# Delta times u in half units, read by groups of 32 rows

## The chip, the cores and the metric

The kernel runs on one core of one Trainium2 chip. The metric is the device time of one execution in microseconds; the time before is 8791.93 us, the median of three runs (8787.54 to 8800.51). A change of about 0.2% is what three such runs can tell from none.

## The reference

The input `x` is 4 images of 96 channels and 64 x 64 pixels, in float32. Four layers follow one another: a selective scan in four directions (layer 0), a deformable 3 x 3 convolution (layer 1), a Fourier mixing and a quantised feed-forward (layer 2), and linear attention with another feed-forward (layer 3). The change is in layer 0. Cut to what matters there:

```python
xs = stack(rows, columns, rows reversed, columns reversed)   # 4 directions k, 192 channels d, 4096 positions
delta = softplus(dts + delta_bias)                           # per k, d and position
def step(h, inp):                                            # h: 16 states n for each k, d
    d_t, u_t, b_t, c_t = inp
    dA = exp(d_t[..., None] * A)
    h = dA * h + (d_t * u_t)[..., None] * b_t[:, :, None, :]
    y = einsum('bkdn,bkn->bkd', h, c_t)
    return (h, y)
_, ys = lax.scan(step, h0, (dl, ul, bl, cl))
y = ys + D * u
```

So for each image, each of 4 directions and each of 192 channels, 16 linear recurrences run over 4096 positions. `delta * u` has one value per channel and position and has to reach all 16 states.

## The kernel before

Layer 0 first computes delta and delta times u for 512 positions at a time, 128 or 64 channels at a time (`steps`, L811 on), and stores them in DRAM (`de_d`, `du_d`). Delta times u is stored as three bfloat16 parts whose sum is the float32 value: L866, L871 and L876 make the parts with the help of two products with minus the identity, and L880 stores them as `[direction, part, channel, position]`.

The scan (`scan`, L884 on) reads them back. Its work is cut into 1536 units. A unit is one image, one direction, 1024 positions and 8 channels x 16 states on the 128 partitions. Eight units make a block of 64 channels (`i` from 0 to 3, `q` from 0 to 1: unit `s = i + 4q` has the 8 channels from `8s`), three blocks make a step, and four steps make an image's direction. For each unit:

- `fetch` (L948) loads delta, each of 8 rows of 4 KB read 16 times, into `da` (L979, from ScalarE's queue), five units ahead.
- `fetch_block` (L991) loads, once per block and some six units ahead, two tiles `du` of 96 partitions (3 parts x 32 channels) and 1024 positions from SyncE's queue (L994). `fetch_step` loads B and C as `bc` (L986).
- `decay` (L998): ScalarE makes exp(A delta) in place (L1000), with a column of `al` as scale.
- `inflow` (L1003): TensorE spreads delta times u over the states. The 96 rows of one `du` tile are multiplied with a matrix `rep` of zeros and ones, 96 x 128, which picks the unit's 8 of 32 channels and adds the 3 parts. Two products of 512 positions fill the two PSUM banks of `db` (L1006). There are two `db` tiles.
- `enter` (L1020): VectorE multiplies `db` by B; `recur` (L1028): VectorE scans; `weigh` (L1035, L1037): GpSimd keeps the last state and multiplies by C.
- `total` (L1056): for two units at a time, TensorE adds the 16 states of each channel with `fold` into `py`, 32 channels at a time; `settle` (L1067) copies `py` to `yb`, `store` (L1074) writes it to DRAM.

Each engine takes its instructions in program order. That order is made when the program is written out: `scan` lays down the units, and between two units a planner (`Clock`, `pipe`, `Stream`) puts in steps of side work: layer 0 of the next image, layers 1 to 3 of earlier ones. A step goes in when the planner's account of each engine says that there is room; the account uses planned costs, such as the 0.8 us of TensorE per unit in `inflow` (L1004). Image 0 is computed by rows first, and its scan starts as soon as the first 1024 positions are there.

DMAs of SyncE and of ScalarE use eight semaphores in turn, in program order; an issue waits until the DMA eight before it has landed.

Of the kernel before, what the change touches and what calls it, by code (L numbers as in the profile page):

```python
# [20 lines left out]
L = H * W  # L21
DI, NS, R, KG = 192, 16, 6, 4
D2 = DI - 128
T = 1024
# [20 lines left out]
def prepare(x, **w):  # L45
# [51 lines left out]
    dtp[64 : 64 + R + 1, 2:] = dtw[2:].transpose(2, 0, 1)  # L97
    a["dtw"] = dtp

    al = w["L0_conv_A_logs"].reshape(KG, DI // D8, D8, NS)  # L100
    a["al"] = c(al.transpose(3, 2, 0, 1).reshape(128, KG * DI // D8))

    ds = w["L0_conv_Ds"].reshape(KG, NG, 64).transpose(2, 1, 0)
    a["ds"] = c(np.concatenate([ds, ds]))
# [22 lines left out]
    for n in (2, 3):  # L127
# [14 lines left out]
    a["cen_c"] = wide(cen[128:], 256)  # L142

    p = np.arange(128)
    rep = (p[:, None, None] % 32 == 8 * np.arange(4)[None, :, None] + p[None, None] % 8).astype(f)
    a["rep"] = c(rep)
    a["fold"] = c(
        (p[:, None, None] % 8 + 8 * np.arange(4)[None, :, None] == np.arange(32)[None, None]).astype(f)
    )
    yy, xx = np.divmod(np.arange(L).reshape(32, 128).T, W)  # L150
    ki, kj = np.divmod(np.arange(9), 3)
# [372 lines left out]
class Unit:  # L524


    def __init__(self, b, k, step, g, i, q):
        self.b, self.k, self.step, self.g, self.i = b, k, step, g, i
        self.s = i + 4 * q
        self.back = k >= 2  # L530
        self.j = NT - 1 - step if self.back else step
        self.n = 8 * g + self.s
        self.key = f"{b}_{k}_{self.j}_{g}_{self.s}"
        self.first_of_block = i == 0 and q == 0
        self.first_of_step = self.first_of_block and g == 0
        self.ts = slice(self.j * T, (self.j + 1) * T)
        self.bc = self.du = None
# [5 lines left out]
class Layer0:  # L543
# [7 lines left out]
    def __init__(self, ctx, net, x1):  # L551
        self.net, self.x1 = net, x1
        tc, nc, ins = net.tc, net.nc, net.ins
        wp = ctx.enter_context(tc.tile_pool(name="l0w", bufs=1))
        for name in ("fold", "al", "ds"):
            setattr(self, name, net.load(name, wp))

        nc.scalar.activation(self.al, self.al, AF.Exp)
        nc.vector.tensor_scalar_mul(self.al, self.al, -1.0)

        dsum = wp.tile([128, NG], F32, name="dsum")
        nc.vector.reduce_sum(dsum, self.ds, axis=mybir.AxisListType.X)
        self.skip = wp.tile([128, NG, 128], F32, name="skip")
        for g in range(NG):
            nc.vector.tensor_scalar_mul(self.skip[:, g, :], net.ident, dsum[:, g : g + 1])

        self.wc_d = net.dram.tile([C, 9, 256], F32, name="wc_d")
        self.rep = wp.tile([128, 4, 128], BF16, name="rep16")
        self.minus = wp.tile([128, 128], BF16, name="minus")
        nc.vector.tensor_scalar_mul(self.minus, net.ident, -1.0)  # L570
        with tc.tile_pool(name="l0prep", bufs=1) as tp:
            nc.vector.tensor_copy(self.rep, net.load("rep", tp))
            w_in = net.load("w_in", tp)
            cw = tp.tile([C, 9, 256], F32, name="cwr")
            nc.sync.dma_start(cw, ins["cw"].partition_broadcast(C))
            nc.vector.tensor_mul(cw, cw, w_in[:, :256].unsqueeze(1).to_broadcast([C, 9, 256]))
            nc.sync.dma_start(self.wc_d, cw)
        dram = net.dram
        self.u_d = [dram.tile([DI, L], F32, name=f"u{b}") for b in range(B)]
        self.z_d = [dram.tile([DI, L], F32, name=f"z{b}") for b in range(B)]  # L580
        self.de_d = [dram.tile([KG, DI, L], F32, name=f"de{b}") for b in range(B)]
        self.du_d = [dram.tile([KG, 3, DI, L], BF16, name=f"du{b}") for b in range(B)]
        self.bc_d = [dram.tile([KG, 2 * NS, L], F32, name=f"bcd{b}") for b in range(B)]
        self.y_d = [dram.tile([KG, DI, L], F32, name=f"y{b}") for b in range(B)]
        self.sp = ctx.enter_context(tc.tile_pool(name="l0s", bufs=2))
        self.banks = ctx.enter_context(ExitStack())
        self.ps = self.banks.enter_context(tc.tile_pool(name="l0q", bufs=1, space=PSUM))


        self.ready, self.summed = set(), set()  # L590

        self.scanned = (0.0, 0.0)

        self.settled = 0.0
# [215 lines left out]
    def steps(self, b, ks, j, us, dtw, sm, xdbl):  # L810
# [65 lines left out]
        nc.scalar.copy(du[:, 2, :], pr)  # L876
        yield cost(pe=0.4, act=0.6)
        for p0, p1, k, c0 in parts:
            dst = self.du_d[b][k][:, c0 : c0 + p1 - p0, cs]
            nc.sync.dma_start(dst.rearrange("s c t -> c s t"), du[p0:p1])  # L880
        self.ready.update((b, k, both, j) for k in ks)
        yield wait(frees="du")

# [66 lines left out]
    def fetch(self, u, before):  # L950


        sp, nc = self.sp, self.net.nc
        b, k, j, g, ts = u.b, u.k, u.j, u.g, u.ts
        c0 = 64 * g
        halves = [slice(j * T + h * CH, j * T + (h + 1) * CH) for h in range(2)]
        if not u.first_of_step:
            u.bc = before.bc
        elif u.bc is None:
            self.fetch_step(u)  # L960
        if u.first_of_step and u.step == 0:
            u.state = sp.tile([128, DI // D8], F32, name=f"st{u.key}", tag="st")
        else:
            u.state = before.state
        if not u.first_of_block:
            u.du, u.sums = before.du, before.sums
        else:
            u.sums = {"add": None}
            if u.du is None:
                self.fetch_block(u)  # L970
        if u.i == 1 and u.s == 1 and (k == 0 or u.back):
            add = u.sums["add"] = sp.tile([128, CH], F32, name=f"ad{u.key}", tag="ad", bufs=1)
            src = self.y_d[b][k - 2] if u.back else self.u_d[b]
            for h in range(2):
                nc.scalar.dma_start(add[64 * h : 64 * h + 64], src[c0 : c0 + 64, halves[h]])
        self.net.clock.add(ACT, 0.6, self.scanned[1])
        u.da = sp.tile([128, T], F32, name=f"da{u.key}", tag="da", bufs=6)
        src = self.de_d[b][k][c0 + D8 * u.s : c0 + D8 * u.s + D8, ts]
        nc.scalar.dma_start(u.da, src.unsqueeze(0).to_broadcast([NS, D8, T]))  # L979

    def fetch_step(self, u):
# [5 lines left out]

    def fetch_block(self, u):

        u.du = []  # L990
        for q in range(2):  # L991
            t = self.sp.tile([96, T], BF16, name=f"du{u.key}_{q}", tag=f"du{q}")
            c0 = 64 * u.g + 32 * q
            self.net.nc.sync.dma_start(t, self.du_d[u.b][u.k][:, c0 : c0 + 32, u.ts])  # L994
            u.du.append(t)

    def decay(self, u):
        u.decayed = self.net.clock.add(ACT, 1.15, 0.0)  # L998
# [1 line left out]
        self.net.nc.scalar.activation(u.da, u.da, AF.Exp, scale=self.al[:, a : a + 1])  # L1000

    def inflow(self, u):
        u.spread = self.net.clock.add(PE, 0.8, self.scanned[1])  # L1003
        db = self.ps.tile([128, 2, CH], F32, name=f"db{u.key}", tag="db", bufs=2)  # L1004
        for h in range(2):
            self.net.nc.tensor.matmul(  # L1006
                db[:, h, :],
                lhsT=self.rep[:96, u.s % 4, :],
                rhs=u.du[u.s // 4][:, h * CH : (h + 1) * CH],
                start=True,  # L1010
                stop=True,
            )
        u.db = db.rearrange("p h t -> p (h t)")
# [848 lines left out]
```

## Time and profile before

| | us |
|---|---|
| median of the runs (lowest, highest) | 8791.93 (8787.54, 8800.51) |
| profiled execution, own time | 8796.72 |
| its span, first to last instruction | 8794.9 |
| VectorE busy | 6862.6 (78%) |
| TensorE busy | 6606.4 (75%) |
| GpSimd busy | 5603.0 (64%) |
| ScalarE busy | 4917.9 (56%) |
| mean granted TensorE clock | 0.813 |

The first unit's multiply starts at 198.3 us and the last scan ends near 7490 us; before it layer 0 of image 0 is prepared, after it the rest of layers 1 to 3 is left. The 1536 scans (L1028, forms with and without an initial state) take 2344 and 2285 ns each, the multiplies by B (L1020) 1213 ns, GpSimd's multiplies by C (L1037) 2386 ns, ScalarE's exponentials (L1000) 1146 ns. Idle time of an engine is put down to what ended it. The chain of work that ended last goes back from the last instruction, at each step to what released it.

### The profile page before, as it was taken

The numbers are of one execution on the slowest core, as the hardware profiler recorded it, in microseconds if no ns is written. First come the engines' busy times: TensorE is split into PE (matmuls) and PEld (weight loads), VectorE is DVE, ScalarE is ACT, GpSimd is POOL, SyncE is SP. The second block draws the span as 40 slices with busy tenths as digits, with TensorE's granted clock in tenths as the row PEclk, the third lists the DMA queues.
The fourth block names the chain that finished last, engine by engine and source line by source line (L and its number), as shares of the span: only waits on it lengthen the run. The fifth ranks groups of instructions, "written<-read, shape, count | busy, mean of one in ns | idle before, by whom it ended". The sixth has DMA issues, their size and how long they took to land.

```text
span 8794.9 us, 96335 instructions
## 1 busy us (share of the span) xinstructions
PE 6606.4 (75%) x31960; PEld 2922.3 (33%) x31960; DVE 6862.6 (78%) x5155; ACT 4917.9 (56%) x9030; POOL 5603.0 (64%) x4291
## 2 busy tenths in 40 slices
PE   6665877679677776877677687777768887779697
PEld 2211221123232322321222354322325552367283
DVE  2799989989798988778899887788887878367414
ACT  4554566546577776655666765345676665322323
POOL 0565666666588887656688886566888776167000
PEclk8876887779788777887778788877888887888887
DMA  3577677877788888777788888766888787255110
GB/s 87 165 199 191 180 194 216 213 185 196 197 234 238 234 225 211 188 186 190 213 237 223 233 221 195 184 167 181 217 209 224 210 219 165 62 164 174 28 52 11
DMA packets 775990, 1608.41 MB, mean 183 GB/s; under 512 B 247809, under 2 KB 339357, under 8 KB 773382
## 3 DMA queue, kind: packets, MB, share of 16 engines
q10 hardware_dynamic: 244224, 843.17, 36.9%
q1 hardware_dynamic: 457542, 532.51, 22.4%
q0 software_dynamic: 73728, 226.57, 9.8%
q8 instruction: 257, 4.21, 0.2%
q14 instruction: 239, 1.96, 0.1%
HBM read 1345.62 MB, written 256.29 MB: 182 GB/s over the span
## 4 chain that ended last, share of the span: by engine, by line
PE 34%; DVE 27%; DMA 17%; ACT 8%; issue 7%; POOL 2%; SPq 2%; ACTq 1%; DVEq 0%; POOLq 0%
DVE hh L1028 13%; DVE db L1020 7%; DMA du<-du 4%; PE pc L750 4%; PE py L1056 4%; PE f L1496 3%; PE ps L1402 3%; DMA da<-de 3%; PE db L1006 3%; ACT g L1381 2%; DMA bc<-bcd 2%; PE pd L1418 2%; ACT da L1000 2%; PE h L1537 1%; POOL hh L1037 1%
## 5 line engine op out<-in xcount | busy, mean ns | idle before, releaser
L1037 POOL TENSOR_TENSOR hh<-hh,bc 128x1024 f32<-128x1024 f32 x1536 | 3661.5, 2386 | 385.4 <-DVE hh L1028 275.6
L1028 DVE TENSOR_TENSOR_SCAN hh<-da,st,db 128x1024 f32<-128x1024 f32 x1152 | 2700.8, 2344 | 183.4 <-PE py L1056 63.9
L1020 DVE TENSOR_TENSOR db<-db,bc 128x1024 f32<-128x1024 f32 x1536 | 1862.9, 1213 | 579.5 <-PE db L1006 577.9
L1000 ACT ACTIVATE da<-da,w_al 128x1024 f32<-128x1024 f32 x1536 | 1740.4, 1146 | 628.8 <-DMA da<-de 207.6
L1006 PE MATMUL db<-du,rep 96*128 96x512 bf16 x3072 | 1093.9, 444 | 899.2 <-DVE hh L1028 853.0
L1369 POOL DMA_INDIRECT g<-table,idx x1152 | 1213.2, 1053 | 366.5 <-issue 179.2
L1056 PE MATMUL py<-hh,w_fold 128*32 128x512 f32 x6144 | 1050.0, 757 | 7.5 <-issue 3.7
L1381 ACT ACTIVATE g<-g,wt 128x96 f32<-128x96 f32 x3456 | 963.8, 364 | 157.6 <-DVE hh L1028 52.4
L1028 DVE TENSOR_TENSOR_SCAN hh<-da,db 128x1024 f32<-128x1024 f32 x384 | 877.3, 2285 | 96.9 <-PE py L1056 43.7
L1006 PEld LDWEIGHTS <-rep 96*128 96x128 bf16 x3072 | 281.2, 106 | 1872.0 <-issue 1195.2
L1402 PE MATMUL ps<-w_ident,g 128*96 128x128 f32 x3744 | 694.4, 328 | 195.8 <-ACT g L1381 130.5
L838 POOL TENSOR_TENSOR lw<-lw,w 128x512 f32<-128x512 f32 x192 | 243.9, 1270 | 722.1 <-DVE w L836 651.0
L1402 PEld LDWEIGHTS ps<-w_ident,g 128*96 128x96 f32 x3744 | 495.7, 145 | 570.3 <-ACT g L1381 258.5
L1035 POOL COPY st<-hh 128x1 f32<-128x1 f32 x1152 | 231.4, 201 | 668.7 <-DVE hh L1028 625.0
L750 PE MATMUL pc<-pad,wc 96*128 96x512 f32 x1152 | 570.7, 629 | 12.2 <-DVE rl L840 3.7
L1410 ACT COPY st<-ps 96x384 f32<-96x384 f32 x384 | 179.7, 474 | 457.6 <-PE ps L1402 415.0
L869 PE MATMUL pr<-ex,w_ident 128*128 128x512 f32 x384 | 281.3, 823 | 152.6 <-DVE ex L859 83.8
L750 PEld LDWEIGHTS pc<-pad,wc 96*128 96x128 f32 x1152 | 220.8, 199 | 320.3 <-issue 284.7
L1056 PEld LDWEIGHTS py<-hh,w_fold 128*32 128x32 f32 x6144 | 154.6, 122 | 493.0 <-issue 367.5
L827 PE MATMUL pd<-xd,w_dtw 103*64 103x512 f32 (+1 forms) x512 | 249.1, 740 | 53.6 <-DVE rl L840 28.4
L1418 PE MATMUL pd<-st,wdc 96*128 96x256 f32 x1152 | 286.5, 396 | 3.6 <-ACT st L1410 1.8
L1505 ACT COPY d<-f 128x512 f32<-128x512 f32 x192 | 111.8, 583 | 305.3 <-PE f L1496 291.2
(252 smaller groups left out, 8829.0 us busy)
## 6 DMA issues: line engine op xcount, KB each, us to landing
da<-de ACTq DMA_DIRECT2D x1536, 512.0 KB
du<-du SPq DMA_DIRECT2D x512, 192.0 KB
bc<-bcd SPq DMA_DIRECT2D x128, 512.0 KB
du<-du SPq DMA_DIRECT2D x128, 384.0 KB
y<-yb SPq DMA_DIRECT2D x384, 128.0 KB
de<-rl SPq DMA_DIRECT2D x128, 256.0 KB
m<-in_dft SPq DMA_DIRECT2D x128, 256.0 KB
ad<-y ACTq DMA_DIRECT2D x192, 128.0 KB
```

Of the source, the lines that this page charges most:

```text
L750: nc.tensor.matmul(pp, lhsT=wc[:, q, g * 128 : (g + 1) * 128], rhs=pad[:, r0 + dy : r0 + dy + NR, dx : dx + W], start=(q == 0), stop=(q == 8),
L869: nc.tensor.matmul(pr, lhsT=net.ident, rhs=ex, start=True, stop=False)
L1000: self.net.nc.scalar.activation(u.da, u.da, AF.Exp, scale=self.al[:, a : a + 1])
L1006: self.net.nc.tensor.matmul(db[:, h, :], lhsT=self.rep[:96, u.s % 4, :], rhs=u.du[u.s // 4][:, h * CH : (h + 1) * CH], start=True, stop=True,)
L1020: self.net.nc.vector.tensor_mul(u.db, u.db, u.bc[:, 0, :])
L1028: nc.vector.tensor_tensor_scan(u.along(u.hh), u.along(u.da), u.along(u.db), first, ALU.mult, ALU.add)
L1037: self.net.nc.gpsimd.tensor_mul(u.hh, u.hh, u.bc[:, 1, :])
L1056: nc.tensor.matmul(py[p0 : p0 + 32], lhsT=self.fold[:, u.i, :], rhs=hc[:, h * CH : (h + 1) * CH], start=u.sums["add"] is None and u.i == 0 ...
L1369: nc.gpsimd.indirect_dma_start(out=g[:, k, :], out_offset=None, in_=self.tables[b % 2], in_offset=bass.IndirectOffsetOnAxis(ap=idx[:, n : ...
L1381: nc.scalar.activation(pixel, pixel, AF.Identity, scale=wt[:, n, c : c + 1])
L1402: nc.tensor.matmul(pt[:, k, :], lhsT=g[:, k, c * C : (c + 1) * C], rhs=net.ident, is_transpose=True, start=(c == 0), stop=(c == corners - 1),)
L1418: nc.tensor.matmul(po, lhsT=wdc[:, k, :], rhs=st[:, k, :], start=(k == 0), stop=(k == 8))
```

## The change

The three parts of delta times u are stored by groups of 32 channels and 512 positions: `[direction, chunk, group, 3 x 32 rows, 512]`, 96 KB in one piece. Each store of 128 or 64 channels becomes four or two stores of 32 channels.

A unit's 8 channels are now every fourth of a group of 32, from `i` on, instead of 8 neighbours. So four neighbouring rows of the stored piece belong to the four units `i`, and a load of 24 partitions with 4 x 512 values each gives every unit its 3 x 8 rows on the same 24 partitions, at another place of the free dimension. A block loads four such pieces, to partitions 0, 32, 64 and 96 of one tile: `q` chooses between the lower and the upper 64 partitions, and the half `h` of the 1024 positions between the two groups of 32 in it.

`inflow` multiplies 24 rows instead of 96, for `h = 0` and `h = 1` in different groups of 32 rows of TensorE, with `rep` as one 128 x 128 matrix. The planned cost goes from 0.8 to 0.5 us. `al`, `fold` and the rows that `da` reads follow the new choice of channels.

```diff
-    al = w["L0_conv_A_logs"].reshape(KG, DI // D8, D8, NS)
-    a["al"] = c(al.transpose(3, 2, 0, 1).reshape(128, KG * DI // D8))
+    al = w["L0_conv_A_logs"].reshape(KG, DI // 32, D8, 4, NS)
+    a["al"] = c(al.transpose(4, 2, 0, 1, 3).reshape(128, KG * DI // D8))
...
-    rep = (p[:, None, None] % 32 == 8 * np.arange(4)[None, :, None] + p[None, None] % 8).astype(f)
-    a["rep"] = c(rep)
+    a["rep"] = c((p[:, None] % 8 == p[None] % 8).astype(f))
     a["fold"] = c(
-        (p[:, None, None] % 8 + 8 * np.arange(4)[None, :, None] == np.arange(32)[None, None]).astype(f)
+        (4 * (p[:, None, None] % 8) + np.arange(4)[None, :, None] == np.arange(32)[None, None]).astype(f)
     )
...
-        self.rep = wp.tile([128, 4, 128], BF16, name="rep16")
+        self.rep = wp.tile([128, 128], BF16, name="rep16")
...
-        self.du_d = [dram.tile([KG, 3, DI, L], BF16, name=f"du{b}") for b in range(B)]
+        self.du_d = [dram.tile([KG, NCH, DI // 32, 3 * 32, CH], BF16, name=f"du{b}") for b in range(B)]
...
         for p0, p1, k, c0 in parts:
-            dst = self.du_d[b][k][:, c0 : c0 + p1 - p0, cs]
-            nc.sync.dma_start(dst.rearrange("s c t -> c s t"), du[p0:p1])
+            for p in range(p0, p1, 32):
+                dst = self.du_d[b][k, j, (c0 + p - p0) // 32].rearrange("(s c) t -> c s t", s=3)
+                nc.sync.dma_start(dst, du[p : p + 32])
...
-        src = self.de_d[b][k][c0 + D8 * u.s : c0 + D8 * u.s + D8, ts]
+        src = self.de_d[b][k][c0 + 32 * u.q + u.i : c0 + 32 * u.q + 32 : 4, ts]
...
-        u.du = []
+        u.du = self.sp.tile([128, 4, CH], BF16, name=f"du{u.key}", tag="du")
         for q in range(2):
-            t = self.sp.tile([96, T], BF16, name=f"du{u.key}_{q}", tag=f"du{q}")
-            c0 = 64 * u.g + 32 * q
-            self.net.nc.sync.dma_start(t, self.du_d[u.b][u.k][:, c0 : c0 + 32, u.ts])
-            u.du.append(t)
+            for h in range(2):
+                p0 = 64 * q + 32 * h
+                src = self.du_d[u.b][u.k, 2 * u.j + h, 2 * u.g + q]
+                self.net.nc.sync.dma_start(u.du[p0 : p0 + 24], src.rearrange("(p i) t -> p i t", i=4))
...
-        u.spread = self.net.clock.add(PE, 0.8, self.scanned[1])
+        u.spread = self.net.clock.add(PE, 0.5, self.scanned[1])
...
-                lhsT=self.rep[:96, u.s % 4, :],
-                rhs=u.du[u.s // 4][:, h * CH : (h + 1) * CH],
+                lhsT=self.rep[64 * u.q + 32 * h : 64 * u.q + 32 * h + 24],
+                rhs=u.du[64 * u.q + 32 * h : 64 * u.q + 32 * h + 24, u.i, :],
```

In the changed kernel the lines of these functions stand three further down (L1006 becomes L1009, L979 becomes L982, L994 becomes L998, L880 becomes L883).

More of the change, by code (lines that the diff above doesn't have):

```diff
@@ L528, in __init__ @@
         self.b, self.k, self.step, self.g, self.i = b, k, step, g, i
+        self.q = q
         self.s = i + 4 * q
```

## The prediction

> **What bounds the kernel now.** I read the page from the top: the busy shares, the chain of work that ended last, the windows by stage, the waits, and then pieces of the chain and of the timeline.
>
> The window from 250 to 7490 us holds nearly the whole scan.
>
> ```profile
> span 8794.9 us, 96335 instructions
> 250.00:7490.00 7240.00, 5385.58 (x24345) 2158.23 (x24348) 6212.86 (x4192) 4393.75 (x8066) 5188.86 (x3937) 0.81 0.78 204
> PE 34%; DVE 27%; DMA 17%; ACT 8%; issue 7%; POOL 2%; SPq 2%; ACTq 1%; DVEq 0%; POOLq 0%
> DVE hh L1028 13%; DVE db L1020 7%; DMA du<-du 4%; PE pc L750 4%; PE py L1056 4%; PE f L1496 3%; PE ps L1402 3%; DMA da<-de 3%; PE db L1006 3%; ACT g L1381 2%; DMA bc<-bcd 2%; PE pd L1418 2%; ACT da L1000 2%; PE h L1537 1%; POOL hh L1037 1%
> ```
>
> VectorE is busy for 6212.86 of 7240 us, so at most 1027 us can be won there. DMA has no compute of its own and still carries 17% of the chain. Next, the waits of VectorE in this window, and the group that it waits for:
>
> ```profile
> DVE db L1020 <- PE db L1006: 534.7, 205, 22.5
> DVE hh L1028 <- PE py L1056: 107.6, 77, 17.7
> L1006 PE MATMUL db<-du,rep 96*128 96x512 bf16 x3072 | 1093.9, 444 | 899.2 <-DVE hh L1028 853.0
> ```
>
> Half of the idle time is for `db`, the product that the change rewrites. The 899 us before it are mostly a wait for VectorE to free a bank, and harmless. The chain itself has, for 1743 us onward:
>
> ```profile
> 1743.25 19.31 DMA du<-du
> 1762.64 0.52 ACTq L979
> 1763.30 0.44 issue
> 1763.87 10.11 DMA y<-yb
> ```
>
> and SyncE's timeline at that place:
>
> ```profile
> 1742.40 1.59 SPq L994 DMA_DIRECT2D du<-du  x2
> 1746.41 2.95 SPq L986 DMA_DIRECT2D bc<-bcd  x2
> 1763.87 5.73 SPq L1074 DMA_DIRECT2D y<-yb  x2
> ```
>
> Nobody needed those `du` tiles at 1763. Over all 384 loads of L994 only the first two land later than TensorE could have used them (17.9 and 5.4 us late); from the 5th percentile up they are 10 us early. What waits is the next DMA on the same semaphore. All DMAs of SyncE and ScalarE share eight semaphores in turn, and each issue waits for the DMA eight before it. I matched issues with semaphore steps: ScalarE is held 159 us by slots of L994 loads and 5 us by slots of L880 stores; SyncE 269 and 28 us. The loads are slow because of their shape: each lands in 3 steps (an L979 load in 16), and takes 10.8 us at the median from issue to landing (20.7 at the 95th percentile) for 192 KB, where L979 moves 512 KB in 6.6.
>
> [...] start to start is 215 ns from `db` to `db` or to another 128-row product and 306 to `py` or a 64-row one, so 91 ns a switch. [...] the trace shows it only for column groups (`py` starts 6 ns apart).
>
> **Part by part.**
>
> *Startup.* The first multiply waits until 198.3 for a load landed at 197.1; `bc` and `da` are there at 189.8 and 190.3. Saved: 8 us (0 to 12).
>
> *Loads.* Two of 192 KB become four of 96 KB per block, 24 rows[...]. The nearest rows are the L880 stores on 16 engines (5.0 us median) and `ad` (4.1); I take 4, or 63% less than 10.8. On the chain in the scan the `du` pieces are 319 us (24 pieces, 13 us each); 0.63 x 319 = 201. In such bursts `bc` and others were issued beside, and become late next; I keep three quarters, 150 us (0 to 201).
>
> *Other DMAs.* Three engines now carry the 75 MB of loads. With a load in flight an L979 has 13 of 16 steps after 5.5 us but the last after 8.0 (4.5 and 5.4 without); a `bc` 7.7 and 17.8 (6.4 and 7.2 without). `da` pieces on the chain are 270 us. Half of the L979 loads meet a `du` load, and of their 8 us 2.5 would go, some 12% of all (32 us); I keep half, 15. `bc` pieces are 183 us; a third of the landing goes (60 us), of which I keep a quarter, 15, since their 1 MB has to move anyway. Together 30 (0 to 92).
>
> *TensorE.* Today a pair takes 0.60 us to its end:
>
> ```profile
> 3017.40 0.60 PE L1006 MATMUL db<-du,rep 96*128 96x512 bf16 x2
> 3017.93 1.06 PE L1056 MATMUL py<-hh,w_fold 128*32 128x512 f32 x8
> ```
>
> Side by side it takes 0.376 plus 0.006 (the `py` step) to 0.106 (if the second weight load is exposed), so 0.38 to 0.48, and 0.09 more where the product before it is a 128-row one. About 0.49 against 0.60, 17%. `db` pieces on the chain are 261 us: 45 us saved. If the pair doesn't overlap, 215 + 106 + two switches cost about as much more. So 45 us saved, between 95 saved and 45 lost.
>
> *Planner.* The cost of 0.8 becomes 0.5, so side work comes earlier: in the built order 4063 instead of 4146 matmuls, and 856 instead of 876 VectorE instructions, follow the last scan. 20 x 0.66 us (578.55 / 876 in the tail) is 13 us moved under the scan; I take 15 us saved in the tail (30 saved to 30 lost, as the scan region gets what the tail gives up).
>
> *More DMAs.* 384 loads and 512 stores are added: 5270 instead of 4374 on eight slots. SyncE is at the head of little, and 896 issues of some 0.45 us lie beside compute. But the DMA eight back is nearer: ScalarE issues with at most one scan between go from 177 to 302, SyncE's from 380 to 809. Behind them stand, on ScalarE, the decays and all side casts, for which TensorE and then VectorE wait; on SyncE, `y` and the next loads. The stores' slots cost 0.1 us (ScalarE) and 0.19 us (SyncE) each at that distance; 1111 x 0.15 = 167 us of queue time, of which I put 70 on the path (0 to 320).
>
> *Hidden.* `fold`, `al`, the split of the store and the smaller `rep` change values or layout, not instructions of compute; `da`'s row pitch I cost at nothing[...] (it hides behind a prefetch of five units[...]).
>
> Sum: 8 + 150 + 30 + 45 + 15 - 70 = 178 us. The span of 8794.9 becomes 8617. The profiled execution took 8796.7, 1.8 around its span, and the median of the runs is 8791.9, 4.8 below it; so 8614 us by the median.
>
> **The rivals.**
>
> *The pair doesn't overlap*[...]: the change then does not do what its layout is for. For it: L801, a 64-row product, repeats at 533 ns where 128-row f32 ones repeat at 428. Against: those stay in one row group. TensorE loses 45 instead of winning it, and the rest stands: 8614 + 90 = 8704.
>
> *Eight slots are too few* (slower). One mechanism: after four stores or four loads in a row, the next `da` or `y` stands behind one that SyncE has barely issued. It decides once the short waits put 248 us (178 + 70) on the path, 0.22 us for each of the 1111 close issues. At 320 us, about 0.29 each, the time is 8614 + 250 = 8864. Against: stores in such slots cost 0.1 to 0.19 us so far; for: 45 ScalarE issues have no scan between (20 before), and each could wait a whole landing of 5 us.
>
> *The transfers were hidden anyway.* If the 319 us pieces only name the last of several equal waits, and the planner's denser side work eats the rest: 8790, no change. For it: much of the idle before L1020 is TensorE held in order behind side work that itself waits for ScalarE and GpSimd.
>
> **How the numbers follow.** Forecast 0.50, no overlap 0.20, hidden 0.08, slots 0.22. A measurement here can tell about 0.2% (18 us) from no change. The first two are faster; of the hidden case most lies within: faster 0.71, same 0.07, slower 0.22. The forecast's own range is 8490 to 8720, by the ends above partly together. For 8 in 10 the range reaches through no overlap and hidden to half of the slots' case: 8440 to 8840.
>
> **What would show it.** Right: the two `db` matmuls start under 110 ns apart and busy time of the group falls from 1094 to about 700 us; `du` loads land in 13 steps[...] within some 4 us; DMA `du` falls from 4% of the chain to about 1%; VectorE's wait for `db` falls under 450 us. Wrong: starts 200 ns apart or more (overlap); ScalarE and SyncE waiting for `du` stores on the chain (slots); a longer landing of L982's `da` (pitch). An undercount would be a chain on which the freed DMAs move all side work up.

## The result

Before, the kernel takes 8789.7 us (median of 4 runs on the chip of the comparison, 8776.7 to 8800.5); changed, 8711.1 us (median of 4, 8681.9 to 8725.7). The ratio is 0.9912, with a 95% interval from 0.9891 to 0.9933: 79 us, or 0.9%, faster. The prediction was 8614 us. Direction and range held; the gain is less than half of the 178 us forecast.

The page of the changed kernel, first the span and the granted clock, then the chain that ended last by engine:

```profile
span 8723.9 us, 97214 instructions
...
PEclk9765787769667777886687788776778887788788
...
PE 25%; DVE 15%; DMA 7%; ACT 5%; issue 4%; SPq 1%; POOL 1%; ACTq 1%; DVEq 0%; POOLq 0%
```

The profiled execution took 8725.7 us, the slowest of the four. The row PEclk gives the TensorE clock in tenths; it has many 6s and 7s (mean 0.779, against 0.813 before). The shares of this chain add up to only about 59%: it was not followed through the whole span, so its 7% of DMA cannot be set against the 17% of before.

The next view gives busy time by stage: stretch, length, then busy us (and instructions) of TensorE, weight loads, VectorE, ScalarE and GpSimd, then granted clock, DMA share and GB/s. The first line is the scan, from the first multiply by B to the end of the last scan; the second is the tail of side work behind it. Before:

```profile
198.00:7491.00 7293.00, 5422.59 (x24444) 2170.30 (x24443) 6252.28 (x4219) 4422.75 (x8100) 5213.98 (x3956) 0.81 0.78 204
7491.00:8795.00 1304.00, 1053.52 (x7244) 700.45 (x7242) 577.55 (x876) 397.17 (x803) 380.00 (x321) 0.83 0.29 82
```

After:

```profile
189.00:7510.00 7321.00, 5515.02 (x24622) 2148.38 (x24621) 6244.21 (x4239) 4456.14 (x8157) 5231.75 (x3964) 0.76 0.80 203
7510.00:8724.00 1214.00, 968.33 (x7064) 661.67 (x7064) 559.27 (x855) 373.37 (x749) 367.92 (x313) 0.85 0.30 87
```

The scan starts 9 us sooner and takes 28 us longer; the tail is 90 us shorter; together 71 us of span. So the stage in which nearly all of the gain was expected got longer. TensorE is busy in it for 5515 us instead of 5423, although its `db` products shrank, as the groups after show:

```profile
L1023 DVE TENSOR_TENSOR db<-db,bc 128x1024 f32<-128x1024 f32 x1536 | 1864.0, 1214 | 604.4 <-PE db L1009 602.7
L1009 PE MATMUL db<-du,rep 24*128 24x512 bf16 x3072 | 710.0, 461 | 858.3 <-DVE hh L1031 803.5
```

L1009 is the old L1006: 710 us busy instead of 1094. Yet VectorE stands still before the multiply (L1023) for 604 us; before it was 579.5. All other TensorE work in the scan grew from 5423 - 1094 = 4329 to 5515 - 710 = 4805 us; it has 178 products more in this stage, and a lower clock.

The waits of VectorE in the whole span after:

```profile
DVE db L1023 <- PE db L1009: 602.7, 262, 26.0
DVE hh L1031 <- PE py L1059: 114.8, 95, 8.1
```

And the loads of `du`, with who waited for them:

```profile
L998 SPq DMA_DIRECT2D du<-du x768: 289/362/10947, 176.1 to 7427.1; - x192
...
  PEld L1009: 27.9, 11
  PE db L1009: 25.9, 6
```

Issuing one takes 0.36 us instead of 0.75, and TensorE waits little for the data. From the semaphore steps in the trace, a load lands in 13 steps (4 before), 5.5 us at the median after its issue (10.9 before; both between 250 and 7100 us), and 9.8 us at the 95th percentile (20.7). `bc` lands 8.5 us after its issue at the median (14.2), `da` 6.0 (6.6). The data moves as predicted; the time did not come back.

### The profile page after: what moved, and what is told of

Same layout as the page of the kernel before. It is cut to its first block, busy times and chain, and to the rows that moved or that the text cites. A ratio compares the mean times of both kernels' runs of the same rounds, so it can differ in the third digit from the quotient of the medians.

```text
span 8723.9 us, 97214 instructions
## 1 busy us (share of the span) xinstructions
PE 6608.9 (76%) x31960; PEld 2859.5 (33%) x31960; DVE 6836.1 (78%) x5155; ACT 4925.0 (56%) x9030; POOL 5608.7 (64%) x4291
## 4 chain that ended last, share of the span: by engine, by line
PE 25%; DVE 15%; DMA 7%; ACT 5%; issue 4%; SPq 1%; POOL 1%; ACTq 1%; DVEq 0%; POOLq 0%
DVE hh L1031 7%; DVE db L1023 4%; PE f L1499 3%; PE ps L1405 3%; PE py L1059 3%; PE pd L1421 2%; DMA da<-de 2%; ACT g L1384 1%; PE db L1009 1%; PE pc L752 1%; PE h L1540 1%; PE yp L1579 1%; DMA m<-in_dft 1%; ACT da L1003 1%; PE lnc L474 1%
## 5 line engine op out<-in xcount | busy, mean ns | idle before, releaser
L1023 DVE TENSOR_TENSOR db<-db,bc 128x1024 f32<-128x1024 f32 x1536 | 1864.0, 1214 | 604.4 <-PE db L1009 602.7
L1009 PE MATMUL db<-du,rep 24*128 24x512 bf16 x3072 | 710.0, 461 | 858.3 <-DVE hh L1031 803.5
L1059 PE MATMUL py<-hh,w_fold 128*32 128x512 f32 x6144 | 1107.7, 796 | 16.2 <-issue 11.5
L1405 PE MATMUL ps<-w_ident,g 128*96 128x128 f32 x3744 | 736.1, 342 | 176.3 <-ACT g L1384 101.2
L1009 PEld LDWEIGHTS <-rep 24*128 24x128 bf16 x3072 | 159.6, 94 | 1963.0 <-issue 1289.7
L871 PE MATMUL pr<-ex,w_ident 128*128 128x512 f32 x384 | 305.7, 889 | 174.7 <-DVE ex L861 81.9
L829 PE MATMUL pd<-xd,w_dtw 103*64 103x512 f32 (+1 forms) x512 | 275.7, 821 | 52.7 <-DVE rl L842 18.8
L1421 PE MATMUL pd<-st,wdc 96*128 96x256 f32 x1152 | 308.9, 419 | 1.3 <-DVE d L1548 1.1
```

What stands on the lines that cost most here:

```text
L871: nc.tensor.matmul(pr, lhsT=net.ident, rhs=ex, start=True, stop=False)
L1009: self.net.nc.tensor.matmul(db[:, h, :], lhsT=self.rep[64 * u.q + 32 * h : 64 * u.q + 32 * h + 24], rhs=u.du[64 * u.q + 32 * h : 64 * u.q ...
L1023: self.net.nc.vector.tensor_mul(u.db, u.db, u.bc[:, 0, :])
L1059: nc.tensor.matmul(py[p0 : p0 + 32], lhsT=self.fold[:, u.i, :], rhs=hc[:, h * CH : (h + 1) * CH], start=u.sums["add"] is None and u.i == 0 ...
L1405: nc.tensor.matmul(pt[:, k, :], lhsT=g[:, k, c * C : (c + 1) * C], rhs=net.ident, is_transpose=True, start=(c == 0), stop=(c == corners - 1),)
L1421: nc.tensor.matmul(po, lhsT=wdc[:, k, :], rhs=st[:, k, :], start=(k == 0), stop=(k == 8))
```

## The experiments

The questions were which part of the change won, and which part lost what it won. One theory puts the missing 100 us on the planned cost (side work drawn into the scan), a rival on the pair of products itself (switches of TensorE's mode, or the lower clock), a third on the 896 added DMAs. Each ratio below is against the kernel before, run on the same chip, with its 95% interval.

### The planned cost alone

```diff
-        u.spread = self.net.clock.add(PE, 0.8, self.scanned[1])
+        u.spread = self.net.clock.add(PE, 0.5, self.scanned[1])
```

> The kernel before with the planned cost of inflow at 0.5 instead of 0.8 and nothing else, so the order of the changed kernel with the old product and the old loads. Theory P (the tail is shorter because the planner moved side work under the scan): the tail after the last scan falls from 1304 to about 1215 us as in the changed kernel; the scan, from 198 to 7491 us before, gets as much longer as the side work needs, 20 to 60 us; the clock stays at 0.81; 8730 to 8770 us. Theory L (the tail is shorter because of the loads and products): the tail stays at 1290 to 1304 us and the time within 20 us of before.

8809.7 us against 8783.6 (medians of 20 and 23 runs), ratio 1.0031 [1.0017, 1.0045]: slower, which neither theory had. The stages of this kernel, and its longest wait of VectorE:

```profile
195.00:7588.00 7393.00, 5494.18 (x24586) 2193.69 (x24621) 6235.13 (x4239) 4452.83 (x8154) 5227.90 (x3963) 0.81 0.76 201
7588.00:8796.00 1208.00, 957.42 (x7066) 652.03 (x7065) 559.88 (x856) 373.38 (x749) 370.20 (x313) 0.86 0.30 87
...
DVE db L1020 <- PE db L1006: 649.1, 272, 31.1
```

The number moved an order of instructions and nothing else. The tail gets 96 us shorter, as theory P said, but the scan gets 100 us longer, not 20 to 60. The side work that moved is some 20 instructions of VectorE, as the prediction counted. Most of what the scan pays is VectorE's wait for `db`, 649.1 us instead of 577.9, most likely because side work that stands earlier also stands ahead of the products that VectorE waits for. The two traces come from different chips and lie within 1 us of each other in all, so the 26 us are read from the medians alone.

### The change with the old planned cost

```diff
-        u.spread = self.net.clock.add(PE, 0.5, self.scanned[1])
+        u.spread = self.net.clock.add(PE, 0.8, self.scanned[1])
```

This edit is on the changed kernel.

> The changed kernel with the planned cost back at 0.8, so the order of the kernel before. Theory C (the pair in two row groups lowers the granted TensorE clock in the scan, and what the pair saves goes to the slower clock): clock 0.76 to 0.78 again, busy time of TensorE no lower than before, scan within 30 us of the 7293 us before, tail 1290 to 1304 us; 8760 to 8800 us. Theory P2 (it was the denser order that held the scan up): the scan shortens by 60 to 150 us against before, clock 0.80 or more; 8640 to 8720 us.

8639.0 us, ratio 0.9841 [0.9811, 0.9872], 72 us below the changed kernel's 8711. Neither theory is right as a whole: the clock in the scan is 0.776, as C said, and the time is about the one that P2 said. Run again on another chip:

> The change at cost 0.8 once more, beside its counterpart with the old product. If the row groups are a loss of their own it is 15 to 40 us slower than that; if they are worth the 45 us of the prediction it is 30 to 60 us faster; within 10 us, saving and switches cancel.

8651.9 us, ratio 0.9866 [0.9851, 0.9881]. So the part of the change that lowers the planned cost takes back 0.5 to 0.7%.

### The wide loads alone

On the kernel before. The parts of `du` are stored as `[direction, channel, part, position]`, so that a load has 96 equal rows; `rep` picks the rows in that order; as many DMAs as before, `inflow` as before.

```diff
-    rep = (p[:, None, None] % 32 == 8 * np.arange(4)[None, :, None] + p[None, None] % 8).astype(f)
+    rep = (p[:, None, None] // 3 == 8 * np.arange(4)[None, :, None] + p[None, None] % 8).astype(f)
...
-        self.du_d = [dram.tile([KG, 3, DI, L], BF16, name=f"du{b}") for b in range(B)]
+        self.du_d = [dram.tile([KG, DI, 3, L], BF16, name=f"du{b}") for b in range(B)]
...
-            dst = self.du_d[b][k][:, c0 : c0 + p1 - p0, cs]
-            nc.sync.dma_start(dst.rearrange("s c t -> c s t"), du[p0:p1])
+            nc.sync.dma_start(self.du_d[b][k][c0 : c0 + p1 - p0, :, cs], du[p0:p1])
...
-            self.net.nc.sync.dma_start(t, self.du_d[u.b][u.k][:, c0 : c0 + 32, u.ts])
+            src = self.du_d[u.b][u.k][c0 : c0 + 32, :, u.ts]
+            self.net.nc.sync.dma_start(t, src.rearrange("c s t -> (c s) t"))
```

> The kernel before with the parts of delta times u stored next to each other per channel, so that a load is 96 equal rows and uses 16 engines, as many DMAs as before, the old product in 128-row mode, cost 0.8. Theory D (the slow loads and their slots cost what the prediction put on them): the loads land in 16 steps within about 6 us, stalls by their slots fall from 430 us to under 100, clock 0.81; 100 to 180 us faster than before, 8610 to 8690. Theory H (those waits were hidden): within 40 us of before, 8750 to 8800, at the same clock.

8552.6 us, ratio 0.9727 [0.9696, 0.9758]: 231 us faster than before on that chip, more than the 100 to 180 of theory D, and the fastest kernel of this study. Each load lands in 16 steps, 5.5 us at the median. First the waits, then the chain of this kernel:

```profile
DVE db L1020 <- PE db L1006: 452.3, 187, 26.4
```

```profile
PE 37%; DVE 32%; DMA 11%; issue 8%; ACT 8%; POOL 2%; SPq 1%; ACTq 1%; DVEq 0%; another core or an unknown queue 0%; POOLq 0%
DVE hh L1028 16%; DVE db L1020 9%; PE py L1056 4%; PE pc L750 4%; PE f L1496 4%; PE ps L1402 3%; PE db L1006 3%; PE pd L1418 2%; DMA da<-de 2%; ACT g L1381 2%; ACT da L1000 2%; PE h L1537 1%; POOL hh L1037 1%; DMA du<-du 1%; PE yp L1576 1%
```

This chain is whole. `du` has gone from 4% to 1%, DMA from 17% to 11%, and the wait for `db` from 577.9 us over the span to 452.3, with the products of `db` untouched. Counted as in the prediction, from the end of the instruction before an issue to the landing of the DMA eight before it, the slots of these loads hold ScalarE for 157 us and SyncE for 272 us before, and for 38 and 2 us here. Other DMAs land sooner too, `bc` after 9.0 us instead of 14.2; how much of the 231 us comes by the slots and how much by these landings isn't separated. In its windows the scan takes 7090 us (7293 before) and the tail 1283 (1304).

### The wide loads with the low planned cost

The edits of the last and of the first experiment together.

> The loads of 96 rows on 16 engines and the planned cost of 0.5, with the old product: the changed kernel without its row groups and without its added DMAs. Theory C: the clock stays at 0.81 and it is faster than the changed kernel, 8590 to 8680 us. If the pair in row groups were worth its 45 us it would be slower than the changed kernel by that: 8740 to 8770 us.

8583.2 us, ratio 0.9770 [0.9742, 0.9799], so 31 us more than the loads alone by the medians; the intervals overlap, the single runs (8528 to 8566 and 8576 to 8593) don't. The scan grows by 86 us and the tail loses 64. So the loss isn't special to the row groups.

### The wide loads with the added DMAs

Like the wide loads, but with each store cut into 32-channel pieces and each load cut in two, so that there are 5270 DMAs as in the changed kernel, of 96 KB each for the loads.

```diff
+            for h in range(2):
+                self.net.nc.sync.dma_start(t[48 * h : 48 * h + 48], src[48 * h : 48 * h + 48])
```

> The loads of 96 rows on 16 engines (old product, cost 0.8), each cut into two of 48 rows, and each store cut into pieces of 32 channels: 5270 DMAs on the eight semaphores instead of 4374, as in the change, with nothing else of it. The change at cost 0.8 stands 86 us above the loads alone (8639 against 8553). Theory S (the added DMAs and their slots cost it): 8610 to 8660 us, clock 0.82. Theory C (the pair in row groups and the clock cost it): 8540 to 8580 us, clock 0.82, though SyncE waits longer for slots.

8614.3 us, ratio 0.9810 [0.9777, 0.9842]. Run again beside two others:

> The loads of 96 rows with the added DMAs, old product, cost 0.8, once more, as the base beside the other two on one chip: 0.981 of the kernel before, as it was (0.978 to 0.984).

8609.7 us, ratio 0.9812 [0.9799, 0.9825]. The added DMAs cost about 0.85%, 62 us by the medians, as theory S said.

This kernel is the changed kernel without its row groups, at the old planned cost. The pair of products can so be read from the two repeats, which ran on the same chip: 8609.7 us without row groups, 8651.9 with them, with intervals that don't overlap (0.9799 to 0.9825, and 0.9851 to 0.9881). The row groups cost about 42 us. Three smaller things differ too: 48 rows per load instead of 24, the row pitch of `da`, and the layout of the stores. Their landings show little of it: at the median 4.7 us for the loads without and 5.3 with, 5.9 and 6.0 for `da`, 4.1 and 4.3 for the stores. The groups without row groups:

```profile
L1024 DVE TENSOR_TENSOR db<-db,bc 128x1024 f32<-128x1024 f32 x1536 | 1862.4, 1213 | 491.7 <-PE db L1010 490.2
L1010 PE MATMUL db<-du,rep 96*128 96x512 bf16 x3072 | 1088.7, 442 | 902.0 <-DVE hh L1032 851.4
```

With them:

```profile
L1023 DVE TENSOR_TENSOR db<-db,bc 128x1024 f32<-128x1024 f32 x1536 | 1862.3, 1212 | 489.8 <-PE db L1009 488.2
L1009 PE MATMUL db<-du,rep 24*128 24x512 bf16 x3072 | 697.1, 452 | 949.1 <-DVE hh L1031 908.5
```

The group of `db` is busy 392 us less, and VectorE waits for it just as long, 490.2 and 488.2 us. The windows of the two scans, without row groups:

```profile
197.90:7317.90 7120.00, 5374.67 (x24419) 2156.24 (x24444) 6255.23 (x4219) 4420.42 (x8100) 5213.94 (x3956) 0.82 0.81 209
```

and with them:

```profile
191.30:7342.50 7151.20, 5330.70 (x24419) 2097.63 (x24443) 6250.73 (x4219) 4419.12 (x8102) 5216.48 (x3956) 0.78 0.82 208
```

The scan is 31 us longer with the same number of products. VectorE's idle time in it rises from 865 to 901 us, most of that ahead of its scans (228.0 to 254.5 us from 190 to 7310); of these the view puts 72 and 85 us down to `py`. All of TensorE is busy only 44 us less, so its other products take 348 us more.

The traces can't place the 42 us more closely. The profiled execution with row groups, 8623.8 us, is the fastest of its four, and in the first pair of traces (8615.0 and 8606.1 us) the two scans take 7131 and 7127 us. What both pairs agree on is that the `db` group is busy 392 and 394 us less, all of TensorE only 44 and 69 us less, and that the clock in the scan falls from 0.819 to 0.781 and from 0.813 to 0.776. Where TensorE's saving goes is the question of the next experiments.

### The two switches

On the wide loads with the added DMAs: after each pair of 96-row products a product of 24 rows and one column, which adds zeros to `db`. It has the new pair's form: it was to bring the two switches, and hardly anything else.

```diff
+        self.net.nc.tensor.matmul(
+            db[:, 1, :1], lhsT=self.none[:24], rhs=u.du[0][:24, :1], start=False, stop=True, skip_group_check=True
+        )
```

> The loads of 96 rows with the added DMAs, old product, cost 0.8, and after each pair one product of 24 rows and a single column that adds zeros: per unit two more changes of TensorE's mode (some 91 ns each) and next to no work, so the cost of the row groups without their gain. Theory M (what the pair saves, some 212 ns, goes into the two switches and their waits): 30 to 100 us slower than the same kernel without it, run beside it. Theory N (switches cost nothing here): within 15 us of it.

8685.5 us, ratio 0.9900 [0.9887, 0.9914], 76 us slower than without it on the same chip, as theory M said. First a stretch of TensorE's timeline before (start, length, instruction):

```profile
3015.89 0.60 PE L1006 MATMUL db<-du,rep 96*128 96x512 bf16 x2
3016.33 1.02 PE L869 MATMUL pr<-ex,w_ident 128*128 128x512 f32 x2
3017.19 0.38 PE L870 MATMUL pr<-du,minus 128*128 128x512 bf16 x1
3017.40 0.60 PE L1006 MATMUL db<-du,rep 96*128 96x512 bf16 x2
```

The same place with the two switches:

```profile
3023.47 0.60 PE L1012 MATMUL db<-du,rep 96*128 96x512 bf16 x2
3024.00 0.17 PE L1019 MATMUL db<-du,none 24*128 24x1 bf16 x1
3024.11 1.13 PE L871 MATMUL pr<-ex,w_ident 128*128 128x512 f32 x2
3025.07 0.38 PE L872 MATMUL pr<-du,minus 128*128 128x512 bf16 x1
3025.28 0.60 PE L1012 MATMUL db<-du,rep 96*128 96x512 bf16 x2
```

And with the change:

```profile
3016.12 0.38 PE L872 MATMUL pr<-du,minus 128*128 128x512 bf16 x1 [0.64 <-ACT du L868]
3016.43 0.51 PE L1009 MATMUL db<-du,rep 24*128 24x512 bf16 x4
```

In the kernel before, `pr` starts 0.44 us after the pair (3016.33 - 3015.89); with a one-column product between them, 0.64 (3024.11 - 3023.47). If both switches are alike, that is some 0.1 us into the mode and 0.1 out of it, with the column's own time. And from `pr` (L870, L872) to the pair it takes 0.21 us before and 0.31 in the change. So the new pair pays a switch with a full-size product on either side. `py`, in groups of 32 columns, pays one with the old pair as well as the new: from `db` to `py` it is 308 ns before and 315 after, start to start, at the median of 466 and 416 at full clock, and from `py` to `db` 525 in both.

The weight loads (PEld, which put the matrix of a product into TensorE) show what stands in this time. Before, around the same pair:

```profile
3017.19 0.31 PEld L1006 LDWEIGHTS <-rep 96*128 96x128 bf16 x2 [0.33 <-issue]
```

With the change:

```profile
3016.43 0.21 PEld L1009 LDWEIGHTS <-rep 24*128 24x128 bf16 x4 [1.44 <-issue]
```

Before, the load for the pair at 3017.40 begins at 3017.19, together with the product ahead of it, and is hidden under that product. In the change it begins at 3016.43, together with the pair itself. This holds for nearly all of them: 17% of the loads of `rep` begin less than 20 ns ahead of a `db` product before, 96% in the change. One such load takes some 0.09 us at the median, so a switch is about as long as a weight load that no longer hides; that the load is what makes it so long was not tried.

By an estimate, most of the 348 us are so accounted for. Counted in the trace of the repeat with row groups, about 754 of the 1536 pairs follow within a microsecond of a full-size product and 389 are followed so by one: 1143 switches of some 95 ns, 109 us. The granted clock in the scan is 0.781 instead of 0.819. The records of the clock know only full and half (356 stretches each in the trace of before), so that is 44% of the scan at half clock instead of 36%. It lengthens the 5375 - 1089 = 4286 us of other products by 206, as if all of their time went with the clock. Together 315 of 348 us. In the kernel with the two switches, where TensorE is busy more, the clock is 0.815: the switches alone hardly lower it.

### A wide product ahead of the pair

On the change with the old planned cost: one product of 128 rows and 512 columns per unit, written into `db` and overwritten by the pair. It gives TensorE the activity back that the pair took away.

```diff
+        wide = self.minus.unsqueeze(1).to_broadcast([128, 4, 128])
+        self.net.nc.tensor.matmul(db[:, 0, :], lhsT=self.minus, rhs=wide, start=True, stop=True)
```

> The change at cost 0.8 with one more product per unit ahead of the pair, a 128-row one of 512 columns into the same bank, which the pair then overwrites: 216 ns and no further result. Theory A: the clock in the scan rises from 0.777 to 0.80 or more, and the time stays within 40 us of the 8639 of the change at cost 0.8, or falls below it. Theory W: clock 0.77 or lower, and 40 to 120 us slower, 8680 to 8760 us.

8668.5 us, ratio 0.9878 [0.9843, 0.9914], against 8639.0 and 8651.9 without it: no gain, some 15 to 30 us more if anything. But the granted clock in the scan is 0.815 instead of 0.776:

```profile
PEclk9876887889788887887787888877788997888898
```

So the lower clock goes with the pair's lower activity: put a product in, and the clock is back. What the clock costs in time stays open, as the extra product costs time itself.

The same on the changed kernel, with its low planned cost:

> The changed kernel as it is, cost 0.5, with one more 128-row product of 512 columns per unit ahead of the pair, overwritten by it. At cost 0.8 the same product raised the granted clock and took 30 us. Theory G: the clock in the scan rises from 0.765 to 0.81 and the denser order becomes cheaper, 8640 to 8711 us, no slower than the change. Theory S, or that the clock is worth nothing here: 8730 to 8770 us, 20 to 60 above the change.

8829.0 us where before took 8852.8 on that chip, ratio 0.9975 [0.9960, 0.9990]; the changed kernel's is 0.9912. The clock rose from 0.763 to 0.806 in the scan, and 0.6% was lost. Raising the clock this way is no remedy.

### The added DMAs with the low planned cost

> The loads of 96 rows on 16 engines, cut into as many DMAs as in the change, planned cost 0.5: all of the change but the products in row groups. The lower cost alone took 27 us on the kernel before, 31 on the loads alone, but 72 on the change (8639 to 8711). Theory G (it is the row groups with their lower clock that make the denser order dear): 8614 + 30 = 8630 to 8660 us, clock 0.82. Theory S (it is the eight slots, which the denser order crowds): 8670 to 8710 us.

On the same chip 8738.9 us, ratio 0.9859 [0.9819, 0.9899], where the old cost gave 0.9810 and 0.9812. This is the changed kernel without its row groups, and its interval lies below that of the changed kernel (0.9891 to 0.9933) but for a small overlap. With the two medians the row groups cost about 0.5% here too, on different chips. Between the two theories it doesn't decide: this chip is slower (8852.8 us before), and by the ratio the time lies between their ranges. The low cost takes 0.5%, some 42 us, without any row groups, so it is not shown that the row groups make it dearer.

### A higher planned cost

On the wide loads, 1.1 us instead of 0.8:

> The loads of 96 rows alone with the planned cost of inflow at 1.1 instead of 0.8: from 0.5 to 0.8 the scan gained 86 us and the tail lost 64. If side work is still too dense: scan 20 to 60 us shorter, tail 10 to 60 us longer, 8520 to 8550 us. If 0.8 is about right: 8560 to 8600 us, the tail taking more than the scan gives.

8654.9 us, ratio 0.9857 [0.9824, 0.9889], 102 us more than the wide loads at 0.8 and beyond both expectations. The stages:

```profile
189.00:7103.00 6914.00, 5178.95 (x22867) 2036.56 (x22908) 6208.30 (x4152) 4331.93 (x7935) 5197.30 (x3924) 0.83 0.82 213
7103.00:8628.80 1525.80, 1226.95 (x8779) 816.28 (x8777) 642.12 (x991) 471.85 (x939) 406.15 (x337) 0.86 0.28 78
```

The scan is 176 us shorter than at 0.8 (7090), the tail 243 longer (1283). Of the three values tried, 0.8 is the best: at 0.5 the scan gets longer by more than the tail gets shorter, at 1.1 the tail gets longer by more than the scan gets shorter.

### Half the product

The second of the two products is left out, and the multiply reads B twice, so that TensorE's part of `inflow` falls to half without row groups. It was meant to give the worth of a shorter pair and the effect of its activity.

> The loads of 96 rows alone, with the second of the two products of inflow left out; the multiply by B reads B twice instead of the product, so that part of the computation is left out. TensorE stays in its mode and is some 216 ns shorter per unit, about what the pair in row groups saves. Theory A (the clock follows TensorE's activity in the last few us, so a shorter product alone lowers it): clock in the scan from 0.82 to 0.77-0.79. Theory W (products in two row groups at once, or the switches of mode, lower it): clock in the scan 0.81 to 0.83. In both the time is 8500 to 8580 us; by A nearer the upper end.

9364.7 us, ratio 1.0669 [1.0632, 1.0706]. The time says nothing on the worth of a shorter pair, for the multiply itself became slower:

```profile
L1020 DVE TENSOR_TENSOR db<-bc 128x1024 f32<-128x1024 f32 x1536 | 2690.4, 1752 | 404.7 <-PE db L1006 403.9
L1035 POOL COPY st<-hh 128x1 f32<-128x1 f32 x1152 | 660.8, 574 | 298.5 <-DVE hh L1028 280.4
```

With both inputs in SBUF it takes 1752 ns instead of 1213: 1536 x 0.539 = 828 us of VectorE, about the 812 us by which this kernel is slower than the wide loads alone. The clock still tells something: in the scan it is 0.765 instead of 0.818 (over the whole execution 0.779 instead of 0.825), with no row groups and no switch added, while TensorE is busy 69% of the scan instead of 76%. So the clock fell along with TensorE's activity, without row groups and without switches. Part of this comes of the longer scan and not of the shorter product.

## Why the prediction was right and wrong

Put in a row, each kernel adds one part to the one before it. The ratios are those above (for the row groups the repeats that share a chip); a difference of ratios times 8790 us gives the microseconds. The second and the last row compare kernels on different chips, each against the kernel before on its own chip, and are good to some 20 to 40 us by the intervals.

| part | ratio, from, to | measured us | predicted us |
|---|---|---|---|
| loads to more engines, with startup and other DMAs | 1 to 0.9727 | -240 | -188 |
| 896 more DMAs | 0.9727 to 0.9812 | +75 | +70 |
| pair in row groups | 0.9812 to 0.9866 | +47 | -45 |
| planned cost 0.5 | 0.9866 to 0.9912 | +40 | -15 |
| sum | 1 to 0.9912 | -77 | -178 |

With the first run of the change at the old cost (0.9841) the last two read +25 and +62; their sum stays.

**Startup.** 8 us were predicted; the first multiply starts at 188.9 instead of 198.3, 9.4 us. Right.

**Loads and other DMAs.** The mechanism was right, and its size 52 us too small. What waited was the next DMA on the same semaphore, and wide loads end that: the slots of the loads hold the two queues for 40 us instead of 429, the kernel with the loads alone has `du` at 1% of the chain and is 231 us faster, so the rival that the transfers were hidden anyway is out. The terms cut down by hand (three quarters of 201, half and a quarter of the others) were where it was undersized; the uncut 201 + 92 + 8 is 301, and the truth of 240 lies between. How many engines a load of 24 rows would reach was the author's estimate. In the traces, of the packets of `du` loads with no other DMA of SyncE beside them, at most 3 run at once in 94% of the time before (27 loads) and at most 12 in 98% of it in the change (89 loads). A landing takes 4 steps before, where the prediction's "3 steps" left one out, 13 in the change, and 16 with 96 equal rows. That `da`'s row pitch of 64 KiB (16 before) would cost nothing was an estimate too, and no cost is seen: 6.0 us to landing at the median, 6.6 before.

**More DMAs.** 70 predicted, 62 by the medians and 75 by the ratios. Right in size, and in part by luck. Counted as above, all slots together hold the two queues for 555 us with the loads alone and for 922 and 979 us with the added DMAs: 370 to 420 us of queue time more, not 167, of which a smaller share than expected reached the path. The rival that eight slots are too few needed 248 us, and is out.

**TensorE.** The failing step is "About 0.49 against 0.60, 17%". That products in two row groups overlap was an estimate from the 6 ns of `py`'s column groups, and the overlap is there: 3 ns from start to start, against 220 before (medians at full clock); the busy time of the group fell to 710 us, as said. The rival of no overlap is out. Two things were missing in the price. It counted the switch on the way in, but not the one out to a full-size product: from the start of a bfloat16 product of 512 columns ahead of a pair to the start of the full-size one behind it, at full clock, the shortest four take 648 to 651 ns before and 628 to 631 in the change. Only with `py` behind does the gain come to the 110 ns of the prediction (742 against 635 at the median). The second is the granted clock. In the trace of before the shortest stretch of one clock takes 3.41 us. In the scan a stretch at half clock follows 3.41 us in which TensorE was busy 38% of the time at the median (321 stretches), one at full clock 3.41 us at 100% (322). A kernel with TensorE busy 75% lies between, and with the shorter pair more of its scan fell to half clock (44% instead of 36% in the repeats), which by the estimate above lengthens the other products by 206 us. Switches and clock together, again by that estimate, take back 315 of the 392 us that the pair gives, and VectorE's wait for `db` didn't change (490.2 and 488.2 us). So the prediction's "45 us saved" put a price on the pair alone and took 17% off the 261 us of `db` on the chain, while the wait for `db` did not move. That the row groups lose 42 us where they should have won 45 is shown, and that added switches cost time is shown too (76 us, with more of them than the change has); how the loss divides between switches and clock stays open.

**Planner.** "I take 15 us saved in the tail" had the wrong sign in sum. The tail did get 96 us shorter in the run of the cost alone, far more than the 15; the scan got 100 longer there, and 86 with the wide loads. The step that failed is to count what leaves the tail and to take its price in the scan as less: with the low cost VectorE's wait for `db` grows from 577.9 to 649.1 us on the kernel before, from 452.3 to 531.4 with the wide loads, from 490.2 to 534.8 with the added DMAs, and on the change from 472.8 and 488.2 (cost 0.8) to 602.7. The sum is a loss of 26 us alone (8783.6 to 8809.7), 31 with the wide loads and 40 to 62 on the change, at the end of the prediction's range (30 lost) or past it; on the change by kernels of different chips.

**The signs that were named.** Starts under 110 ns apart, the busy time near 700 us and 13 steps: seen. Landing "within some 4 us": 5.5. DMA `du` at 1% of the chain: not readable in the profile after, whose chain covers too little, but seen with the loads alone. VectorE's wait for `db` under 450 us: 565.3 between 250 and 7490 us, where 534.7 were read before, and 602.7 over the whole span. It is the one sign that spoke of the sum, and it failed. At the old cost the two runs have 452 and 435 us there, so it is the planned cost that made it fail. "An undercount would be a chain on which the freed DMAs move all side work up" named something else than what happened. The 77 and the 178 us differ by three terms: 52 more from the loads, 92 less from the pair and 55 less from the planner, beside 5 for the DMAs. That the time still lies in the prediction's range is in part luck: the loads gave more than forecast and hid about a third of what the pair and the planner lost.

## What to carry to other kernels

Price an instruction with its neighbours, from the start of the one before to the start of the one behind: a shorter group gains next to nothing where each switch of form (here about 0.1 us) costs what overlap saves. Ask what a shorter job does to the granted clock of an engine that is busy three quarters of the time (here 0.819 to 0.781), and don't let a planner's cost follow a measured duration without trying values on both sides. Here the best of the change was one layout edit, the load that lands in 16 steps instead of 4, with no DMA added: 8552.6 us alone, where the whole change has 8711.1.

## What the runs showed of the hardware

- A switch of TensorE's mode, between a product of 96 or 128 rows and one of 24 rows or of 32 columns, cost about 91 to 100 ns from start to start (306 ns against 215 ahead of `py`, 0.31 us against 0.21 ahead of the pair); with a product of a single column in between, there and back, it was 0.2 us. In the change 96% of the pair's weight loads, some 0.09 us each, began only with the pair; before, most began a product earlier, 216 ns ahead at the median.
- The mean granted clock in the scan went from 0.819 to 0.781 when 392 us of `db` products were saved; one more 512-column product per unit took it from 0.776 to 0.815 in another pair of kernels. Two switches per unit left it at 0.815.
- Beside `du` loads that land in 4 steps `bc` landed after 14.2 us at the median, beside loads that land in 16 steps after 9.0 (the kernel before and the wide loads alone, between 250 and 7100 us).
- VectorE's multiply took 1752 ns with both inputs in SBUF and 1213 with one in PSUM; beside it GpSimd's copy of the state took 574 ns instead of 201.
